# A graph network kernel: background list work moved from the ends of layers and the first attention batches into the steady stretches of layers 1 and 2

## The chip, the cores and the metric

The kernel runs on one core of a Trainium2 chip. The metric is device microseconds of one execution, lower is better. The inputs and the result lie in HBM. The engines are TensorE (PE; its weight loads are shown as PEld), VectorE (DVE), ScalarE (ACT), GpSimd (POOL) and SyncE (SP). Each engine works through its own queue of instructions in order. Plain DMAs are issued from the queues of SyncE and ScalarE; gathers and scatters by an index (indirect DMAs) are issued from GpSimd, one instruction for each 128 rows.

## The reference

A graph of 50000 nodes with 64 features and 25000 edges, sorted by target, goes through four layers. Each layer is `x = x + layer(relu(layernorm(x)))`.

```python
h = relu(layernorm(x)); m = relu(concat(h[src], h[dst]) @ W_msg + b_msg)        # layer 0
x = x + relu(concat(h, segment_mean(m, dst)) @ W_upd + b_upd)
h = relu(layernorm(x)); m = h[src] * (deg**-.5)[src] * (deg**-.5)[dst]          # layer 1
x = x + (segment_sum(m, dst) + h) @ W.T + b
h = relu(layernorm(x)); q, k, v = h @ Wq + bq, h @ Wk + bk, h @ Wv + bv         # layer 2, 4 heads
logits = sum(q[dst] * (k[src] + ek[type])) * scale + es[type] + clip(log(eg[type]))
agg = segment_sum((v[src] + ev[type]) * segment_softmax(logits, dst), dst) @ Wo + bo
y = layernorm(h + film(agg)); x = x + layernorm(y + gelu(y @ W1 + b1) @ W2 + b2)
h = relu(layernorm(x)); x = x + expm_multiply(h, src, dst, edge_weight, t)      # layer 3
```

Layer 3 applies a matrix exponential of the sparse edge matrix: 4 substeps of a Taylor series of 20 terms each.

## The kernel before, in words

**Tiling.** Nodes are cut into 49 batches of 1024 (`NQ`); the edges of a batch are put in 640 slots, five tiles of 128. Within a layer every batch goes through a list of stages (small Python functions), and the batches are staggered: in each round every batch that is under way runs its next stage, and then a new batch begins. Class `Steps` (from line 82) does a round, `pipeline` (line 110) repeats rounds until all 49 batches are through.

- Layer 0 (line 2229): `fetch, hots, message, sums, update, project`. `fetch` issues five gathers on GpSimd (`ga`), `project` ends with `g` (line 2222), which goes to the table `g1tab` in HBM.
- Layer 1 (line 2282): `fetch, scaled, sums, turn, product`. `fetch` issues five gathers `gt` from `g1tab`, into four buffers; `sums` adds the result to `x` (`x2`, line 2255); `product` writes the keys and values to `kvtab`.
- Layer 2 (lines 2499 to 2510): a pipeline `up` (`fetch, hots, logits`; five gathers `kvg` from `kvtab`) and a pipeline `down` of twelve stages, beginning with `fetch2, message, sums` and ending with `close`, which writes `h3tab`. The 49 batches form four groups (13, 12, 12, 12). First `up` runs alone over group 0, then a softmax over the group; after that `up` of the next group and `down` of the groups before it alternate. When all four softmaxes are done, `down` alone runs to its end.
- Layer 3 (from line 2631): a first power of the edge matrix, a second one, and then the powers 3 to 8 on short lists of edges, added to the output by GpSimd.

All of `g1tab`, `kvtab` and `h3tab` must be written before the next layer's first gather, since a batch may need any node.

**The list work.** The powers of layer 3 need, for each power k from 2 to 8, a list of those edges that continue a path. `build_lists` (from line 1920) is a Python generator that emits the instructions for these lists in small steps (`yield`). List 2 consists of 49 steps of five one-hot comparisons each (`lhot`, line 1791, VectorE, with nine small matmuls into a PSUM tile `lp`, line 1795), seven copies out of PSUM, 24 steps that mark nodes (line 1724), and 98 look-ups (`lgot`, one indirect DMA on GpSimd each). VectorE reads the look-ups in `llv` (lines 1733 and 1734). List 3 consists of 98 steps of one one-hot each (line 1878), eleven groups of key comparisons (`link`, line 1597), a marking (`map_three`) and 42 look-ups. Lists 4 to 8 are shorter, and each is a chain of scatter, reading back, comparing, scatter, look-up. `lhot` and `lp` have one buffer each. The whole is some 605 steps.

**How list work is let go.** An object `Pace` (line 121) hands it out. After every stage of a batch, the pipeline calls its hook; a call adds `rate` to a credit, and for each whole credit one step of the list work is emitted. Where a step yields "wait" (a DMA must land before the next), the credit is set to `-gap * rate`. `pipeline` can be given an `edge`: with `first=False`, the hook is used as long as batches are still begun, and once all 49 are begun each stage lets go `edge.edge` steps instead.

```python
        if edge:
            full = s.begun < len(items) and (not first or len(s.at) >= len(stages) - 1)
            s.hook = hook if full else lambda: edge(edge.edge)
```

In layer 0 the hook is another `Pace` called `work` (rate 0.1): weights of later layers, and `load_slots`, which loads the columns from which the lists start. It has 21 steps, which the first 210 of the 294 stages use up.

**Order of instructions.** The code gives an order, and the framework decides at build time the order in each engine's queue: an instruction whose inputs are ready can be put ahead of earlier code where its engine is planned to be idle. The queues on the chip are in order. So the position of a step in the code sets its rank, and not strictly its place.

Of the kernel before, what the change touches and what calls it, by code (L numbers as in the profile page):

```python
# [52 lines left out]
BK, NQ, RG = 392, 49, 98  # L53
# [56 lines left out]
def pipeline(items, stages, hook=None, edge=None, first=True):  # L110

    items = list(items)
    s = Steps(items, {q: State() for q in items}, stages, hook)
    while s.done < len(items):
# [3 lines that stand above are left out]
        s.step()  # L118
# [855 lines left out]
def fast(ctx: ExitStack, tc: tile.TileContext, a: dict, out: bass.AP, flag: bass.AP):  # L974
# [946 lines left out]
    def build_lists():  # L1921

        yield from list_two(cols)
        yield from list_three(lists[2])
        for k in range(4, KD + 1):
            q = lists[k - 1]
            yield from compact(k, q.live[:, :q.n], q.n, (q.src, q.dst, q.w.bitcast(I32), q.nextptr))

    lists_pace = Pace(build_lists())
# [77 lines left out]
    def halves(w, a0, a1, pool, name):  # L2007

        out = []
        for h in range(2):  # L2010
            t = pool.tile([P, D], F32, name=f"{name}{h}")
            nc.scalar.dma_start(t[0:D, :], (a0, a1)[h])
            nc.scalar.dma_start(t[D:P, :], (a1, a0)[h])
            out.append(t)
        return out
# [145 lines left out]
    with tc.tile_pool(name="l0c", bufs=1) as cp, tc.tile_pool(name="l0", bufs=2) as pool, \  # L2161
            tc.tile_pool(name="pl0", bufs=1, space=PSUM) as ps:
        wupd = halves(None, a["L0_gnn_W_upd"][D:2 * D, :], a["L0_gnn_W_upd"][0:D, :], cp, "wupd")
        bupd = bias_rows(cp, row_bcast("L0_gnn_b_upd", pool=cp), "bupd")
        w1t = cp.tile([P, P], F32, name="w1t")
        nc.vector.memset(w1t, 0.0)
        for h in range(2):
            nc.scalar.dma_start(w1t[h * D:(h + 1) * D, h * D:(h + 1) * D], a["L1_gnn_WT"])

        def fetch(q, s):  # L2170
            s.ga = pool.tile([P, 5, D], F32, name="ga", bufs=4)
            for i in range(5):
                gather(s.ga[:, i, :], atab, nrs[:, q, i:i + 1])
            s.bt = pool.tile([P, 8, BW], BF16, name="bt", bufs=4)
            nc.sync.dma_start(s.bt, nodes(btab, q))
            s.cat = pool.tile([P, 2, 512], F32, name="cat", bufs=5)
            load_turned(s.cat, h0t, q)
            s.xt = pool.tile([P, 8, D], F32, name="xt", bufs=6)
            load_x(s.xt, q)
            load_keys(pool, q, s)  # L2180

        def hots(q, s):
            node_hot(pool, s)
            s.soh = slot_hot(pool, key, q)

        def message(q, s):
            pe = ps.tile([P, 5, D], F32, name="pe", bufs=2)
            to_slots(pe, s, s.bt)
            z = pool.tile([P, 5, D], F32, name="z")
            nc.vector.tensor_add(z, s.ga, pe)  # L2190
            m3 = pool.tile([P, 5, 3, D], F32, name="m3")
            for i in range(5):
                nc.scalar.activation(m3[:, i, 0, :], z[:, i, :], AF.Relu, scale=cinv[:, q, i:i + 1])
            s.parts = split(m3)

        def sums(q, s):
            pa = ps.tile([P, 512], F32, name="pa")
            to_sums(pa, s.soh, s.parts)
            for h in range(2):
                r = slice(h * D, h * D + D)  # L2200
                nc.scalar.activation(s.cat[r, h, :], pa[r, :], AF.Copy)

        def update(q, s):
            po = ps.tile([P, 8, D], F32, name="po")
            bias_in(po.rearrange("p b d -> p (b d)"), bupd)
            for j in range(8):
                nc.tensor.matmul(po[:, j, :], s.cat[:, j // 4, j % 4 * P:j % 4 * P + P], wupd[j // 4],
                                 start=False, stop=(j == 7))
            s.x1 = pool.tile([P, 8, D], F32, name="x1", bufs=3)
            nc.vector.scalar_tensor_tensor(s.x1, po, 0.0, s.xt, op0=OP.max, op1=OP.add)  # L2210
            s.h = pool.tile([P, 8, D], F32, name="h")
            norm_relu(pool, s.h, s.x1)

        def project(q, s):
            tr = turned(pool, ps, s.h, "pt")
            pw = ps.tile([P, 8, D], F32, name="pw", bufs=2)
            for i in range(4):
                nc.tensor.matmul(pw[:, 2 * i:2 * i + 2, :].rearrange("p a d -> p (a d)"), tr[:, i, :], w1t,
                                 start=True, stop=True)
            g = pool.tile([P, 8, D], F32, name="g")  # L2220
            nc.vector.tensor_add(s.x1, s.x1, pw)
            nc.vector.tensor_mul(g, pw, over(disn[:, 8 * q:8 * q + 8], 8))
            nc.scalar.dma_start(nodes(x1tab, q), s.x1)
            nc.sync.dma_start(nodes(g1tab, q), g)

        work = Pace(itertools.chain(weights(), load_slots()), 0.1)
        next(work.work)
        lists_pace.edge = 5.0
        pipeline(range(NQ), (fetch, hots, message, sums, update, project), work, lists_pace, False)

# [1 line left out]
    with tc.tile_pool(name="l1", bufs=2) as pool, \  # L2234
            tc.tile_pool(name="pl1", bufs=1, space=PSUM) as ps:
        def fetch(q, s):
            s.gt = pool.tile([P, 5, D], F32, name="gt", bufs=4)
            for i in range(5):
                gather(s.gt[:, i, :], g1tab, nrs[:, q, i:i + 1])
            s.x1 = pool.tile([P, 8, D], F32, name="x1", bufs=4)  # L2240
            nc.sync.dma_start(s.x1, nodes(x1tab, q))

        def scaled(q, s):
            s.soh = slot_hot(pool, key, q)
            g3 = pool.tile([P, 5, 3, D], F32, name="g3")
            for i in range(5):
                nc.scalar.activation(g3[:, i, 0, :], s.gt[:, i, :], AF.Copy, scale=dise[:, q, i:i + 1])
            s.parts = split(g3)

        def sums(q, s):  # L2250
            po = ps.tile([P, 8, D], F32, name="po")
            bias_in(po.rearrange("p b d -> p (b d)"), b1l)
            to_nodes(po, s.soh, s.parts, started=True)
            x2 = pool.tile([P, 8, D], F32, name="x2")
            nc.vector.tensor_add(x2, s.x1, po)
            nc.scalar.dma_start(nodes(x2tab, q), x2)
            s.h2 = pool.tile([P, 8, D], F32, name="h2")
            norm_relu(pool, s.h2, x2)

        def turn(q, s):  # L2260
            s.tr = turned(pool, ps, s.h2, "pt")

        def product(q, s):
            kv = pool.tile([P, 8, 3 * D], F32, name="kv")
            q3 = pool.tile([P, 8, 3, D], F32, name="q3")
            for k in range(2):
                for h in range(2):
                    r = slice(h * D, h * D + D)
                    b = slice(4 * k + h, 4 * k + 4, 2)
                    pp = ps.tile([P, 2, 4 * D], F32, name="pp", bufs=4)  # L2270
                    for i in range(2):
                        nc.tensor.matmul(pp[:, i, :], s.tr[r, 2 * k + i, :], wkv[r, :], start=True, stop=True)  # L2272
                    nc.scalar.activation(kv[:, b, :], pp[:, :, :3 * D], AF.Copy)
                    nc.scalar.activation(q3[:, b, 0, :], pp[:, :, 3 * D:], AF.Copy)
            qt = pool.tile([P, 8, 3, D], BF16, name="qt")
            pack(q3, qt)
            nc.sync.dma_start(nodes(kvtab, q), kv[:, :, :2 * D])
            nc.sync.dma_start(nodes(h2tab, q), kv[:, :, 2 * D:])
            nc.scalar.dma_start(nodes(qtab, q), qt.rearrange("p b k d -> p b (k d)"))

        lists_pace.rate = 0.4
        pipeline(range(NQ), (fetch, scaled, sums, turn, product), lists_pace, lists_pace, False)


    with tc.tile_pool(name="l2", bufs=2) as pool, \
# [209 lines left out]
            nc.vector.scalar_tensor_tensor(h, s.xc, 0.0, over(invert(s, "r3"), 8), op0=OP.max, op1=OP.mult)  # L2495
            nc.scalar.dma_start(nodes(h3tab, q), h)

        lists_pace.rate, lists_pace.gap = 0.7, 5
        up = Steps(range(NQ), S, (fetch, hots, logits), lists_pace)
        down = Steps(range(NQ), S, (fetch2, message, sums, attend, spread1, turn, hidden, product, spread2, finish, spread3,  # L2500
                                      close), lists_pace)
        for k, (q0, n) in enumerate(batches):
            while up.done < q0 + n:
                up.step()
                if k:
                    down.step(q0)
            softmax(k)
        lists_pace.rate = 1.5
        while down.done < NQ:
            down.step(NQ)  # L2510
# [163 lines left out]
    sums = {}  # L2674
# [112 lines left out]
```

## Time and profile before

| what | value |
|---|---|
| runs | 3559.2, 3567.95 and 3574.22 us, median 3567.95 us |
| profiled execution, its own time | 3569.77 us |
| its span, first to last instruction | 3568.0 us |
| VectorE busy | 2620.7 us (73%), 8434 instructions |
| TensorE busy | 2492.4 us (70%) |
| GpSimd busy | 2070.2 us (58%), 1955 instructions |
| ScalarE busy | 1328.5 us (37%) |
| mean granted TensorE clock | 0.693 |
| layer 0's gathers `ga` | 656.9 to 1074.1 us |
| layer 1's gathers `gt` | 1185.6 to 1685.7 us |
| layer 2's gathers `kvg` | 1740.4 to 2471.0 us |
| layer 3's first gathers | from 2767.5 us |

The span is cut by these gathers into layers. A layer's length is the time from its first gather to the next layer's first gather. Busy shares are means over stretches with different limits, so the stretches are read one by one.

### The profile page before, as it was taken

The numbers are of one execution on the slowest core, as the hardware profiler recorded it, in microseconds if no ns is written. First come the engines' busy times: TensorE is split into PE (matmuls) and PEld (weight loads), VectorE is DVE, ScalarE is ACT, GpSimd is POOL, SyncE is SP. The second block draws the span as 40 slices with busy tenths as digits, with TensorE's granted clock in tenths as the row PEclk, the third lists the DMA queues.
The fourth block names the chain that finished last, engine by engine and source line by source line (L and its number), as shares of the span: only waits on it lengthen the run. The fifth ranks groups of instructions, "written<-read, shape, count | busy, mean of one in ns | idle before, by whom it ended". The sixth has DMA issues, their size and how long they took to land. (4 is left out here: it accounts for less than half of the span.)

```text
span 3568.0 us, 62333 instructions
## 1 busy us (share of the span) xinstructions
PE 2492.4 (70%) x21184; PEld 1729.4 (48%) x21184; DVE 2620.7 (73%) x8434; ACT 1328.5 (37%) x2962; POOL 2070.2 (58%) x1955
## 2 busy tenths in 40 slices
PE   7898675399987673477669779889888554356620
PEld 3324565266665452355446445555554443356520
DVE  9999998699998882488677877777878576456410
ACT  0002553144442262377204326646667333333000
POOL 0377777655550477665374127665430787775786
PEclk9755555699996575688657667777779775567555
DMA  1003783487771362478654234343233646377221
GB/s 54 6 4 90 205 234 123 110 224 212 211 200 44 90 197 75 130 234 243 188 145 124 62 90 132 111 122 110 80 94 101 211 139 193 96 216 213 45 26 12
DMA packets 530638, 463.35 MB, mean 130 GB/s; under 512 B 281171, under 2 KB 387954, under 8 KB 530180
## 3 DMA queue, kind: packets, MB, share of 16 engines
q1 hardware_dynamic: 365012, 269.33, 26.5%
q10 hardware_dynamic: 93408, 139.47, 11.3%
q0 software_dynamic: 71888, 50.46, 7.6%
q8 instruction: 169, 2.77, 0.3%
q14 instruction: 161, 1.32, 0.1%
HBM read 226.23 MB, written 233.89 MB: 129 GB/s over the span
## 5 line engine op out<-in xcount | busy, mean ns | idle before, releaser
L1013 POOL DMA_INDIRECT kvg<-kvtab,nrs x245 | 260.6, 1064 | 307.6 <-DVE es L2329 184.0
L1013 POOL DMA_INDIRECT gt<-g1tab,nrs x245 | 243.6, 994 | 238.6 <-DVE lhot L1791 110.6
L1013 POOL DMA_INDIRECT y<-h3tab,sptr x245 | 276.8, 1130 | 138.9 <-issue 68.0
L1013 POOL DMA_INDIRECT ga<-atab,nrs x245 | 250.3, 1022 | 170.4 <-DVE z L2190 60.5
L1991 PEld LDWEIGHTS <-soh 128*128 128x128 bf16 x4410 | 221.7, 117 | 237.0 <-issue 221.8
L1013 POOL DMA_INDIRECT raw<-otab,nrd x196 | 193.4, 987 | 191.9 <-DVE bad L1159 132.5
L1981 PE MATMUL pa<-soh,m 128*64 128x256 bf16 (+3 forms) x1764 | 238.9, 348 | 25.2 <-DVE m L1093 11.6
L1018 POOL DMA_INDIRECT stab<-raw,pf x196 | 207.3, 1058 | 59.8 <-issue 59.8
L1013 POOL DMA_INDIRECT lgot<-nmap,ldst x183 | 190.1, 1039 | 75.3 <-issue 52.8
L1991 PE MATMUL po<-g,soh 128*128 128x64 bf16 x2205 | 123.3, 215 | 145.5 <-DVE g L1093 143.0
L1950 DVE TENSOR_SCALAR soh<-it,key 128x512 bf16<-128x512 f16 (+2 forms) x735 | 210.7, 332 | 1.8 <-PE pa L1981 1.6
L1991 PE MATMUL po<-y,soh 128*128 128x64 bf16 x2205 | 122.3, 228 | 125.9 <-DVE y L1093 65.4
L2272 PE MATMUL pp<-wkv,tr 64*128 64x256 f32 x784 | 151.2, 496 | 52.4 <-ACT tr L2001 52.1
L1013 POOL DMA_INDIRECT y<-ftab,ldst x140 | 138.9, 992 | 75.0 <-issue 45.7
L1093 DVE TENSOR_TENSOR y<-y 128x320 f32<-128x320 f32 (+1 forms) x196 | 75.6, 389 | 140.6 <-ACT y L2617 116.3
L1942 DVE TENSOR_SCALAR noh<-keys,pblk 128x256 bf16<-128x256 f16 (+1 forms) x784 | 176.0, 286 | 2.8 <-DMA keys<-ktab 2.7
L1196 PE MATMUL pab<-wab,tr 64*128 64x128 f32 x784 | 150.3, 437 | 32.5 <-ACT tr L1183 32.5
L1981 PEld LDWEIGHTS <-m 128*64 128x64 bf16 x1764 | 118.0, 119 | 97.9 <-issue 32.5
L1196 PEld LDWEIGHTS pab<-wab,tr 64*128 64x128 f32 x784 | 136.3, 324 | 51.5 <-ACT tr L1183 51.5
L2338 PE MATMUL pe<-qt,noh 128*128 128x64 bf16 x2205 | 157.7, 231 | 0.3 <-DVE noh L1942 0.2
L2720 POOL DMA_INDIRECT out<-y,lnode x85 | 132.4, 1558 | 38.3 <-issue 24.4
L2617 ACT ACTIVATE y<-y,swgt 128x64 f32<-128x64 f32 x245 | 82.2, 345 | 176.6 <-DMA y<-h3tab,sptr 161.1
(607 smaller groups left out, 7496.8 us busy)
## 6 DMA issues: line engine op xcount, KB each, us to landing
kvtab<-kv SPq DMA_DIRECT2D x49, 512.0 KB
ftab<-f ACTq DMA_DIRECT2D x98, 256.0 KB
xt<-in_x SPq DMA_DIRECT2D x96, 256.0 KB
btab<-bt ACTq DMA_DIRECT2D x49, 384.0 KB
bt<-btab SPq DMA_DIRECT2D x49, 384.0 KB
qtab<-qt ACTq DMA_DIRECT2D x49, 384.0 KB
qt<-qtab SPq DMA_DIRECT2D x49, 384.0 KB
xs<-xstab SPq DMA_DIRECT2D x70, 256.0 KB
```

What stands on the lines that cost most here:

```text
L1013: return nc.gpsimd.indirect_dma_start(out=dst, out_offset=None, in_=tab[:, :], in_offset=IndirectOffsetOnAxis(ap=idx, axis=0))
L1018: return nc.gpsimd.indirect_dma_start(out=tab[:, :], out_offset=IndirectOffsetOnAxis(ap=idx, axis=0), in_=src, in_offset=None, bounds_chec ...
L1093: nc.vector.tensor_sub(x3[:, :, k, :], x3[:, :, k - 1, :], h[:, :, k - 1, :])
L1196: nc.tensor.matmul(pab[:, i, :], s.tr[r, i, :], wab[r, :], start=True, stop=True)
L1942: nc.vector.tensor_scalar(s.noh[:, j, :n * P], s.keys[:, t0 * P:(t0 + n) * P], pblk[:, j:j + 1], None, op0=OP.is_equal)
L1950: nc.vector.tensor_scalar(oh[:, OHW[i]:OHW[i + 1]], it16[:, b0 * P:(b0 + n) * P], keys[:, q, i:i + 1], None, op0=OP.is_equal)
L1981: nc.tensor.matmul(o, l, r, start=(k == 0), stop=(k == len(t) - 1))
L1991: nc.tensor.matmul(po[:, j, :], oh[:, c:c + P], msg[:, i, k, :], start=(not started and i == t0 and k == 0), stop=(end and (not started or ...
L2272: nc.tensor.matmul(pp[:, i, :], s.tr[r, 2 * k + i, :], wkv[r, :], start=True, stop=True)
L2338: nc.tensor.matmul(pe[:, i, :], s.noh[:, j, c:c + P], s.qt[:, j, k, :], start=False, stop=(j == b0 + nb - 1 and k == 2))
L2617: nc.scalar.activation(y3[:, i, 0, :], s.y[:, i, :], AF.Copy, scale=swgt[:, 5 * q + i:5 * q + i + 1])
L2720: st = nc.gpsimd.indirect_dma_start(out=out[:, :], out_offset=IndirectOffsetOnAxis(ap=s.node[:, t:t + 1], axis=0), in_=sums[k][:, t, :], i ...
```

## The change

Three rules for the list work are altered; no instruction is added or removed.

- At the end of layer 0 nothing of it is let go any more: `pipeline` gets no `edge`, and its hook is `work` to the end.
- In layer 1 the rate is 0.6 for each stage instead of 0.4, from the first to the last stage, and the last stages no longer let go five steps each.
- In layer 2 the rate is 0 during the first group and 0.75 afterwards, instead of 0.7 throughout. The rate of 1.5 once the four softmaxes are done stays.

```diff
         work = Pace(itertools.chain(weights(), load_slots()), 0.1)
         next(work.work)
-        lists_pace.edge = 5.0
-        pipeline(range(NQ), (fetch, hots, message, sums, update, project), work, lists_pace, False)
+        pipeline(range(NQ), (fetch, hots, message, sums, update, project), work)
...
-        lists_pace.rate = 0.4
-        pipeline(range(NQ), (fetch, scaled, sums, turn, product), lists_pace, lists_pace, False)
+        lists_pace.rate = 0.6
+        pipeline(range(NQ), (fetch, scaled, sums, turn, product), lists_pace)
...
-        lists_pace.rate, lists_pace.gap = 0.7, 5
+        lists_pace.rate, lists_pace.gap = 0.0, 5
         up = Steps(range(NQ), S, (fetch, hots, logits), lists_pace)
...
             softmax(k)
+            lists_pace.rate = 0.75
         lists_pace.rate = 1.5
```

## The prediction

> **What bounds the kernel now.** I read the strip of 40 slices first. It shows that no engine holds the whole span.
>
> ```profile
> DVE  9999998699998882488677877777878576456410
> POOL 0377777655550477665374127665430787775786
> ```
>
> VectorE (DVE) is at 8 or 9 in layer 0, but falls to 2 and 4 in slices 15 and 16 (1338 to 1516 us), where GpSimd (POOL) reads 6 and 7. Then I asked for the busy time by stretch, cut at the layers' ends. Columns: stretch, length, then busy us and instructions of PE, PEld, DVE, ACT, POOL; clock, DMA.
>
> ```profile
> 1094.00:1186.00 92.00, 68.10 (x547) 47.67 (x542) 74.30 (x318) 11.96 (x28) 0.38 (x1) 0.55 0.09 32
> 1186.00:1237.00 51.00, 32.32 (x326) 22.73 (x326) 41.48 (x183) 13.14 (x36) 38.67 (x40) 0.51 0.30 85
> 1237.00:1313.00 76.00, 64.69 (x636) 47.36 (x637) 67.97 (x198) 53.65 (x159) 48.66 (x43) 0.75 0.71 210
> 1313.00:1473.00 160.00, 43.83 (x404) 34.49 (x402) 41.88 (x103) 36.18 (x108) 119.84 (x126) 0.57 0.27 76
> 1473.00:1716.00 243.00, 176.48 (x2044) 141.39 (x2043) 208.79 (x499) 180.71 (x557) 134.21 (x135) 0.86 0.78 233
> ...
> 1740.00:1836.00 96.00, 65.37 (x792) 49.84 (x792) 62.62 (x286) 1.51 (x4) 74.21 (x71) 0.50 0.66 190
> ...
> 2545.00:2717.00 172.00, 154.24 (x806) 92.97 (x806) 140.20 (x475) 119.35 (x190) 48.03 (x45) 0.84 0.31 92
> ```
>
> Row 5 is layer 1 undisturbed: VectorE 86% busy, 31.8 batches in 243 us, so 7.64 us a batch with 1.1 us of VectorE idle. Row 1 is layer 0's end, row 2 layer 1's start, row 4 something that is not VectorE at all. The tile views say what. First the one-hots of list 2, then the look-ups `lgot`, and below them the gathers `gt`, in the stretches 1237 to 1313, 1313 to 1473 and 1473 to 1690.
>
> ```profile
> L1791 DVE TENSOR_SCALAR lhot<-it,lpos x245: 234/282/475, 1104.9 to 1204.9; 128x256 bf16<-128x256 f16 x123
> ...
> POOL gt L1013: 110.6, 1
> ```
>
> ```profile
> 1237.00:1313.00 76.00, 0.00 (x0) 21.38 (x18) 0.75 0.71 210
> 1313.00:1473.00 160.00, 0.21 (x1) 76.81 (x81) 0.57 0.27 76
> ```
>
> ```profile
> 1313.00:1473.00 160.00, 10.27 (x30) 43.03 (x45) 0.57 0.27 76
> 1473.00:1690.00 217.00, 47.11 (x139) 134.21 (x135) 0.87 0.80 238
> ```
>
> ```profile
> DVE llv L1733 <- DMA lgot<-nmap,ldst: 71.8, 1, 71.8
> ```
>
> The 245 one-hots lie across the change from layer 0 to layer 1. The look-ups stand between gathers, 81 to 45 in row 4's stretch: 126 indirect DMAs at 1.25 us each (0.95 busy, 0.30 to the next, by the timeline) make 158 of the 160 us. GpSimd is the bound there, and VectorE sits 71.8 us before `llv`, the last line, quoted from the waits of that stretch.
>
> **How many steps move.** Counting the code's credits through both versions gives, for layer 0's end, layer 1, layer 2's first group, the other groups, the end of `down`, layer 3: before 75, 132, 29, 282, 88, 0; after 0, 145, 0, 320, 140, 0. List 8 is done at the very end of layer 2 instead of 57 stages before that. Dense work of layer 3 begins at the same batch.
>
> **Part 1, layer 0's end.** `g` (line 2222) comes every 8.7 us up to 1096.5 us, and the last four at 1129.4, 1153.5, 1170.9 and 1181.7. In these 92 us the list's VectorE instructions, each counted to the start of the next, make 48.2 us, the rest 26.2, idle 17.6. Without the list, four more at 8.7 end at 1131: 50 us gained. Bounds: 60 if the end is limited by the 26 us left, 35 if the build fills the idle stretches with list work whose waits for `lp` stay. I take 48.
>
> **Part 2, list 2's VectorE work in layer 1.** It is 48.2 at layer 0's end, 26.8 in row 2 and 7.7 in row 3: 83 us. Some 18 us still find idle time (17.6 at layer 0's end, 9 at layer 1's start, less the waits). The other 65 go beside full batches. Row 3 prices that: nine batches in 75.6 us, 6.8 over nine times 7.64, for 7.7 us of list work, 0.9 for 1. So 58 us, of which today's layer 1 pays 23 (row 2: `x2` of batch 2 is 50 us after the first gather, where 13 to the first and 7.64 twice make 28) and 7. Loss: 28 us. Bounds by far rows: at 0.5, a loss of 2; at 1.5, the price of `link` and `map_three` (1991 to 2128 us: 137 us for four batches that take 17 each elsewhere, so 69 for 46.7 us of list work), a loss of 68.
>
> A rule speaks against this part. The Trainium skill, SBUF — State Buffer, section "Who interferes with whom", says that a `tensor_scalar` can run in a mode that takes a port pair which GpSimd needs to write its descriptors, and the later one blocks. The trace: beside 54 one-hots a gather took 0.967 us (row 2, 38.67 for 40), 0.956 in row 4 with VectorE mostly idle (43.03 for 45), 0.994 in row 5's. If each of the 245 blocked GpSimd for its whole 0.28 us, an estimate by the rule would be 69 us of GpSimd time; by these rows it is nothing that counts.
>
> **Part 3, the 98 look-ups.** The code before spreads them at two a batch from batch 7 to the end of layer 1. The trace has them at ten a batch, in 1278 to 1464 us: the build pulled them forward into GpSimd's idle places. The batches 13 to 17 took 153 us instead of 38: 115 us lost, about 98 times 1.25 less GpSimd's slack. After, the code has 57 of them from batch 28 of layer 1 on, three a batch, and 41 in layer 2. I expect them to be pulled forward again, as soon as list 2 is marked, ten a batch, with the same loss. Value 0; bounds: a gain of 68 (rival 1), a loss of 10.
>
> **Part 4, layer 1's end and the first group.** The 16 one-hots of list 3 leave the end of layer 1, where the last `qt` is 12 us behind the one before it instead of 7.6: 5 us gained (0 to 11). In the first group GpSimd's five gathers, 6.7 us a batch, end last (74.21 of 96 us busy, 0.30 between two), and VectorE has a third idle (row 6). So the 29 steps there cost nothing now, and 46 steps of list 3 (23 one-hots in the trace's first group, 7.5 us, 19 in the end of layer 1, 5.8 us, and their copies, some 4) go beside VectorE work of 17 us a batch: 15 us lost (0 to 25).
>
> **Part 5, `down`'s end.** 25 waits of lists fall there instead of 20. Today's thirteen batches take 13.2 us each, where those without list work lie 10.5 apart: 35 us, 1.75 a wait, 9 us for five. As many leave the groups before (12 to 8 waits): 7 back. Loss 2. Nothing hides the last steps, as `h3tab` must be complete for layer 3. Behind VectorE's reading of a look-up stand `finish` and `close` of the last batches; bounds 5 gained, 25 lost.
>
> **The sum.** −48 +28 +0 −5 +15 +2 = −8, so 3561 us from the profiled execution's own 3569.8 (its span and 1.8 around it, and 1.8 above the median of the runs). A measurement of this kernel can tell about 0.5% from no change, 18 us; this forecast lies within.
>
> **Rival 1, faster: the look-ups spread as the code has them.** If list 2's marking is late, its look-ups meet the end of layer 1 and the 53 us between the last `gt` and the first `kvg`, in which GpSimd is empty. Then 57 cost 71 us less 28 of slack, and 41 cost nothing: 43 instead of 111, and 3493 us. For it: three a batch is slow. Against: before, the look-ups ran at five times the rate of the code.
>
> **Rival 2, slower: list work in layer 1 at the price of `link`.** `lhot` and `lp` have one buffer, so each step goes from VectorE to TensorE and back, through two queues full of layer 1's work; whoever stands behind the waiting one-hot on VectorE (`ln_s`, `ln_xc`, `h`, and so `tr`, `pp`) waits with it. At 1.5 per us the 65 us cost 98, and the time is 3601. It decides from 1.2 on. For it: 1991 to 2128 us. Against: row 3, where marking by the same buffers cost 0.9.
>
> **Rival 3: it hardly does what it says.** The build pulls list 2 into the same idle places at layer 0's end, and all else with it: 3568.
>
> **How the numbers follow.** The forecast's case has 0.50, with 3535 to 3590 as its own range: 0.12 faster than 3550, 0.33 within, 0.05 slower than 3586. Rival 1 has 0.18, all faster; rival 2 0.25, all slower; rival 3 0.07, 0.06 of it within. Together 0.30, 0.39 and 0.31. The range reaches to both rivals with the outer part of each left out, and takes in the bounds of parts 3 and 5: 3505 to 3612.
>
> **What would show it.** Right: the first `gt` near 1138 us instead of 1185.6; batches of layer 1 10 us apart while list 2's one-hots run; 98 `lgot` in a block of some 150 us late in layer 1, ended by one long wait of `llv`; first group unchanged at 6.7 us a batch. Wrong: one-hots still ahead of the first `gt`; `lgot` in layer 2; batches over 12 us apart beside the one-hots; a first layer 3 gather that waits for a list.

## The result, and the profile after

| | before | changed |
|---|---|---|
| runs (median) | 3568.71 us | 3612.39 us |
| profiled execution, its own time | 3569.77 us | 3620.12 us |
| its span | 3568.0 us | 3618.2 us |
| mean granted TensorE clock | 0.693 | 0.688 |

The ratio is 1.012, with an interval of 1.0099 to 1.0141: 44 us slower, where 3561 had been forecast, and 0.4 us above 3612, the top of the range. Some of the experiments ran on chips where the kernel before itself takes 4674 to 4755 us and undisturbed batches of layer 1 lie 11.3 to 11.5 us apart; their numbers are marked "slower chips" below, and stand only against the kernel before beside them.

The layers, cut at the first gathers as before:

| us | before | changed | undone part 1 (`l0_back`, below) |
|---|---|---|---|
| up to the first `gt` | 1185.6 | 1132.6 | 1187.5 |
| layer 1, to the first `kvg` | 554.8 | 628.7 | 552.7 |
| layer 2, to the first `y` | 1027.1 | 1061.3 | 1010.2 |
| the rest | 800.5 | 795.7 | 794.7 |

Layer 0's end gave 53 us, layer 1 took 74 and layer 2 took 34. The strip of the changed kernel's page, the same two lines as before:

```profile
DVE  9999998699998777824677768787777576556310
POOL 0377777655553534676474211675352687765786
```

VectorE reads 7 in the slices 13 to 15 (1176 to 1447 us), where before had 8, 8 and 2. The hole of 2 and 4 is two slices later, and GpSimd's 7 and 6 with it. The stretches, columns as before (length, busy us and instructions of PE, PEld, DVE, ACT, POOL; clock, DMA share, GB/s):

```profile
1095.00:1133.00 38.00, 27.16 (x216) 19.52 (x215) 35.07 (x104) 10.98 (x27) 0.43 (x1) 0.80 0.22 76
1133.00:1198.00 65.00, 44.53 (x500) 33.56 (x500) 49.40 (x150) 35.74 (x106) 49.76 (x51) 0.67 0.59 170
1198.00:1442.00 244.00, 212.55 (x1643) 139.22 (x1642) 177.50 (x597) 117.82 (x347) 104.41 (x102) 0.56 0.52 149
1536.00:1677.00 141.00, 29.44 (x245) 22.30 (x246) 28.22 (x71) 25.30 (x74) 107.17 (x112) 0.57 0.22 57
```

Row 1 is layer 0's end: 38 us instead of 92. Row 4 is the look-ups' stall, with GpSimd as the bound: 141 us for four batches, 110 more than four times 7.64, where before lost 115. Row 3 is new. It is the stretch beside list 2's steps, as long as row 5 of before (243 us), but with 19 batches in place of 31.8: 12.8 us a batch, and 13.2 while the one-hots themselves run (14 batches in 1199 to 1384 us). VectorE is no longer full there (73%, against 86%). TensorE is busy for 87%, with a clock of 0.56 against 0.86. The tile views of list 2's one-hots and look-ups, and the wait that ends the look-ups:

```profile
L1791 DVE TENSOR_SCALAR lhot<-it,lpos x245: 230/281/434, 1125.9 to 1383.3; 128x256 bf16<-128x256 f16 x123
```

```profile
L1013 POOL DMA_INDIRECT lgot<-nmap,ldst x98: 940/944/1436, 1487.4 to 1669.8; - x98
```

```profile
DVE llv L1733 <- DMA lgot<-nmap,ldst: 81.6, 1, 81.6
```

The one-hots start where layer 0 ends and run for 257 us instead of 100. The look-ups still stand in a block, and VectorE still waits for its end. What VectorE waits for in 1199 to 1384 us (sum, times, longest):

```profile
DVE lhot L1791 <- PE lp L1795: 27.3, 20, 2.5
DVE ln_v L1138 <- ACT ln_sq L1151: 21.1, 13, 2.4
DVE lkey L1799 <- PE lp L1795: 3.7, 3, 2.5
```

For 31 us the next one-hot, or the copy behind a group, waits for TensorE's list matmuls into `lp`. Before has no such wait in its undisturbed stretch, which holds next to no list work.

The waits of the other engines in row 3 lead to TensorE too:

```profile
POOL gt L1013 <- ACT g L2246: 104.6, 17, 12.1
ACT kv L2272 <- PE pp L2271: 80.5, 56, 2.7
```

ScalarE's copies `kv` wait 80.5 us for TensorE's product `pp`. The gathers wait 104.6 us until ScalarE's `g` has freed their buffer, 5.5 us a batch. In the undisturbed stretch of before they wait 1.2 a batch for it (39.6 us), and no copy waits for `pp`. So the batches of row 3 wait for TensorE at two places, VectorE for `lp` and ScalarE for `pp`.

### The profile page after: what moved, and what is told of

The parts are those of the page before. It is cut to its first block, busy times and chain, and to the rows that moved or that the text cites. A ratio compares the mean times of both kernels' runs of the same rounds, so it can differ in the third digit from the quotient of the medians.

```text
span 3618.2 us, 62349 instructions
## 1 busy us (share of the span) xinstructions
PE 2534.7 (70%) x21184; PEld 1745.6 (48%) x21184; DVE 2618.7 (72%) x8434; ACT 1325.6 (37%) x2955; POOL 2061.2 (57%) x1955
## 5 line engine op out<-in xcount | busy, mean ns | idle before, releaser
L1013 POOL DMA_INDIRECT y<-h3tab,sptr x245 | 267.9, 1093 | 92.8 <-issue 70.4
L1981 PE MATMUL pa<-soh,m 128*64 128x512 bf16 (+3 forms) x1764 | 230.6, 344 | 29.9 <-DVE m L1093 13.0
L2271 PE MATMUL pp<-wkv,tr 64*128 64x256 f32 x784 | 218.8, 559 | 29.5 <-ACT tr L2001 29.4
L2271 PEld LDWEIGHTS pp<-wkv,tr 64*128 64x128 f32 x784 | 127.7, 265 | 60.2 <-ACT tr L2001 44.5
L2337 PE MATMUL pe<-qt,noh 128*128 128x64 bf16 x2205 | 150.0, 227 | 0.3
```

Of the source, the lines that this page charges most:

```text
L1013: return nc.gpsimd.indirect_dma_start(out=dst, out_offset=None, in_=tab[:, :], in_offset=IndirectOffsetOnAxis(ap=idx, axis=0))
L1981: nc.tensor.matmul(o, l, r, start=(k == 0), stop=(k == len(t) - 1))
L2337: nc.tensor.matmul(pe[:, i, :], s.noh[:, j, c:c + P], s.qt[:, j, k, :], start=False, stop=(j == b0 + nb - 1 and k == 2))
```

## The experiments

Three explanations of the 13 us a batch are set against each other. Hand-off: VectorE's one-hots and TensorE's list matmuls wait for each other through the one buffer between them. Clock: the list's small matmuls lower TensorE's granted clock, and TensorE then bounds the batches, with or without a hand-off. Plain load: VectorE only has more to do.

**The changed kernel again, and part 1 undone.** Two kernels on one chip. The first is the changed kernel as it is:

> The changed kernel as it is, beside the kernel before on one more chip: where the kernel before takes about 3569 us, 1.010 to 1.014 as first measured. The runs so far had 4736 us for the kernel before, with TensorE's results reaching VectorE and ScalarE later than the trace of before has them. On such a chip the clock theory (layer 1 lost its time since TensorE fell to half clock beside list 2's steps) expects less than +20 us, since layer 1's undisturbed batches take 11.3 us there anyway and TensorE has nothing to lose; the price of the hand-off or of plain VectorE load expects the +44 us or more to stay.

It ran where the kernel before takes 3573 us: 3611.22 us, ratio 1.0109 (1.0092 to 1.0126). Its profile repeats the first one (layer 1 627.9 us, layer 2 1058.6); what the change does on a slower chip, it could not show. The second has layer 0's end as before and all else as changed:

```diff
-        pipeline(range(NQ), (fetch, hots, message, sums, update, project), work)
+        lists_pace.edge = 5.0
+        pipeline(range(NQ), (fetch, hots, message, sums, update, project), work, lists_pace, False)
```

> The changed kernel with part 1 undone: five steps a stage beside layer 0's end again, so that list 2's one-hots and most flags are done before layer 1. Layer 1 (three steps a batch, none at its end) and layer 2 (none in the first batch, then 0.75) stay as changed. Layer 0's end then costs its 50 us again, and layer 1's 18 batches at 13 us are gone. Clock or hand-off theory, on a chip like that of the first traces: layer 1 gets shorter by 65 to 90 us, the kernel by 15 to 40 against the changed one, so 3575 to 3600. By the prediction's own terms (layer 0's end -48, VectorE work +28): slower than the changed kernel by about 20 us.

Measured: 3546.92 us, 0.9929 of before (0.9912 to 0.9945), and 64 us below the changed kernel. This is more than any theory had, and the sign of my own terms was wrong. The table above has its layers. Against the second profile of the changed kernel, on the same chip, it has 57 us more up to the first `gt`, 75 less in layer 1 and 48 less in layer 2. So part 1 costs twice: in layer 1, and again in layer 2. The same kernel beats both: what is left of the change (no list work in layer 2's first group, 0.6 in layer 1 to its last stage, 0.75 later) gains 26 us.

**Real steps, no steps and dummies in one layer.** The changed kernel, in which layer 1 has 35 dummy steps behind list 2's one-hots, after six batches without. A dummy step has the same instructions, but its comparisons go into a tile that nobody reads, and its matmuls take a constant. Both are held to a place, behind the last `x2` and the last bias matmul.

```diff
+        yield from itertools.chain(itertools.repeat(None, 18), load(True, True))
         has = lw.tile([P, CAP[2]], F32, name="lhas")
...
+                with tc.issue_after(latest["vector"].ins):
+                    for i in range(5):
+                        hot = lc.tile([P, 2 * P], BF16, name="dhot")
+                        nc.vector.tensor_scalar(hot, it16[:, :2 * P], pidx, None, op0=OP.is_equal)
...
+                            nc.tensor.matmul(po[:, 2 * (q % PG) + o, :], hotc[:, o * P:(o + 1) * P], hotc[:, :NF],
+                                             start=(i == o), stop=(i == 4))
```

> The changed kernel, and in the same layer 1 behind list 2's one-hots, after six batches without list steps, 35 dummy steps at the same three a batch: five comparisons on VectorE and nine narrow matmuls on TensorE each, nothing passing between them, before the flags and look-ups go on. It adds some 12 batches of load, and all later list steps come later; to be read are three stretches of the same layer, not the total: batches beside real steps, batches without, batches beside dummies. Hand-off theory: the dummies' batches are shorter than the real steps' by 2 us or more. Clock theory, or plain load: both the same within 0.7 us; then the clock theory has TensorE over 85% busy in both and its granted clock under 0.65 where undisturbed batches had 0.86, plain load has VectorE over 85% busy and the clock kept.

It took 3659.21 us, beside 3567.93 for before. The three stretches of its layer 1, in the order real steps, none, dummies:

```profile
1199.00:1386.00 187.00, 161.40 (x1339) 107.66 (x1340) 141.77 (x476) 93.48 (x276) 86.38 (x84) 0.61 0.54 156
1386.00:1440.00 54.00, 41.38 (x521) 32.48 (x519) 53.09 (x152) 41.42 (x124) 33.20 (x32) 0.77 0.82 234
1440.00:1573.00 133.00, 101.43 (x1139) 79.19 (x1137) 119.64 (x391) 77.83 (x234) 70.63 (x70) 0.73 0.65 187
```

They hold 15, 7 and 13 batches by the `x2` additions: 12.5, 7.7 and 10.2 us a batch (the first 22 dummy comparisons already run at the end of the second stretch). VectorE's load of list work per batch is the same. The real stretch has 40.5 us of list work on VectorE (2.7 a batch), the other 36.2 (31.5 of 153 dummies and 4.7 of the list's own, 2.8 a batch). Over batches of 7.64 us that makes 72.4 us for 40.5, or 1.8 per us, with the hand-off, and 33.7 for 36.2, or 0.93 per us, without it. VectorE's waits in the first and the third stretch:

```profile
DVE lhot L1791 <- PE lp L1795: 23.5, 20, 2.7
DVE ln_v L1138 <- ACT ln_sq L1151: 15.5, 11, 2.3
DVE lkey L1799 <- PE lp L1795: 3.6, 3, 2.5
...
DVE x L2283 <- PE po L2020: 9.2, 10, 1.4
DVE ln_v L1138 <- ACT ln_sq L1151: 2.5, 6, 1.3
```

Its waits for the list's own matmuls are 27.1 us in 15 batches, 1.8 a batch. Beside the dummies 1.4 us of such waits are left in all, for the few marking steps of the list itself. The batches differ by 2.2 us. This is the hand-off theory's forecast (2 us or more), and my clock theory, by which the load alone lowers the clock, falls for this chip: the same load without the hand-off leaves the clock at 0.73, near the 0.77 without list work, and VectorE is 90% busy. The clock of 0.61 goes along with the hand-off. How much of the 2.2 us the low clock adds, by letting TensorE's matmuls end later, is not separated here: the waits of ScalarE's `kv` for `pp` fall as well, from 57.7 us in 15 batches to 30.0 in 13. The dummies are also held to their place, which the real steps are not, and what that does by itself was not tried. All three stretches are from one execution.

**The two loads one by one (slower chips).** On the changed kernel list 2's steps were finished beside layer 0 (six a stage), and 49 dummy steps took their place in layer 1. First both loads, then the comparisons alone, then the matmuls alone:

```diff
+        lists_pace.work = itertools.chain(itertools.repeat(None, 15), load(True, True), lists_pace.work)
         lists_pace.rate = 0.6
```

> This kernel takes list 2's one-hots and flags out of layer 1: they are finished at the end of layer 0, six steps to a stage. In their place layer 1 runs 49 dummy steps, three a batch as in the changed kernel, each with five 128x256 comparisons on VectorE into a tile that nobody reads, and nine 128x128x7 matmuls on TensorE with a constant one-hot. So both engines have the load of list 2's steps, and nothing passes from one to the other. Three theories on why layer 1's batches went from 7.64 to 13.4 us apart beside list 2's steps, at a granted clock of 0.56 in place of 0.86. Clock: the steps' narrow matmuls slow the stream until the granted clock falls, and TensorE at half clock becomes the bound; it needs no hand-off, so here the batches lie over 12 us apart with the clock under 0.65. Hand-off: the comparisons and matmuls wait for each other through the one buffer between them, which is gone here, so the batches lie at 9.5 to 10.5 us, the clock at 0.75 or more. Plain VectorE load (2.6 us a batch): 10.2 us or so as well, VectorE above 85% busy.

> As the kernel with both dummy loads, but only the five 128x256 comparisons a step stay, three steps a batch; the dummy matmuls are left out. Clock theory: without the extra matmuls the stretch stays near the undisturbed one, 8 to 10.5 us a batch, the clock above 0.7; if the gaps that VectorE's load leaves on TensorE are enough to drop the clock, 12 us or more. Hand-off: 9.5 to 10.5 us. Plain VectorE load: 7.64 + 2.6 = 10.2 us, the same as with both dummies.

> As the kernel with both dummy loads, but only the nine narrow matmuls a step stay (27 a batch, and one 14-column copy to seven steps); the dummy comparisons are left out. Clock theory: the granted clock falls below 0.65 and the batches lie over 10 us apart though VectorE has hardly any added work. Hand-off and plain VectorE load: 7.6 to 8.2 us a batch, clock about 0.85, since 27 matmuls of some 60 ns are 1.6 us on an engine that is 5.55 us busy in 7.64.

Totals 4742.69, 4766.1 and 4735.86 us, beside 4674.26 for before. The batches of a stretch beside the dummies lie 13.5 us apart with both loads (10 batches, 2091 to 2226 us), 13.7 with the comparisons (12 in 164 us), 11.5 with the matmuls (12 in 138 us), and 11.3 with none (15 in 170 us). The stretches with the comparisons alone, and of the third kernel with the matmuls and with neither:

```profile
2099.00:2263.00 164.00, 76.63 (x793) 62.18 (x792) 113.59 (x375) 72.85 (x217) 59.78 (x60) 0.75 0.47 138
```

```profile
2070.00:2208.00 138.00, 88.73 (x1121) 74.22 (x1121) 83.15 (x211) 71.52 (x217) 59.79 (x60) 0.73 0.56 164
2264.00:2434.00 170.00, 98.40 (x990) 81.11 (x990) 101.11 (x241) 89.19 (x270) 74.63 (x75) 0.74 0.57 166
```

So the narrow matmuls cost almost nothing and keep the clock (0.73 against 0.74), and the comparisons cost 2.3 us a batch, though VectorE is only 69% busy with them. With both loads the clock reads 0.63 in its stretch, and the batches are still no longer than with the comparisons alone. Since the undisturbed batches are longer there, this does not settle the question for the first chips. Three more runs of the kernel with both loads, on other slower chips:

> The same kernel as d_free (dummy comparisons and dummy narrow matmuls, nothing passing between them, in the place of list 2's one-hots in layer 1), to be read against the profiles of before and after: batches of 7.64 us at clock 0.86 without list work, 13.4 us at 0.56 with list 2's steps. Clock theory: over 12 us a batch, clock under 0.65, TensorE over 85% busy. Hand-off: 9.5 to 10.5 us, clock 0.75 or more, since there is none here. Plain VectorE load: about 10.2 us, VectorE over 85% busy.

> The dummy loads (five comparisons a step on VectorE, nine narrow matmuls a step on TensorE, three steps a batch, nothing passing between them; list 2's own steps are done beside layer 0's end) once more, where the kernel before takes about 3570 us. Undone part 1 gave 0.993 of before, 65 us off the changed kernel: the time is lost beside list 2's steps in layer 1. Clock theory: the dummies do the same, batches over 12 us apart, clock under 0.65, TensorE over 85% busy. Hand-off theory: 9.5 to 10.5 us and clock 0.75 or more, since here nothing is handed over. Plain VectorE load: about 10.2 us, VectorE over 85% busy.

> The dummy loads of list 2's steps with nothing handed over (five comparisons on VectorE and nine narrow matmuls on TensorE a step, three steps a batch, list 2's own steps done beside layer 0's end), to be read where the kernel before takes about 3570 us and undisturbed batches of layer 1 take 7.64 us at clock 0.86; there list 2's real steps made them 13.4 us at 0.56. Clock theory: over 12 us a batch, clock under 0.65, TensorE over 85% busy. Hand-off theory: 9.5 to 10.5 us and clock 0.75 or more. Plain VectorE load: about 10.2 us, VectorE over 85% busy.

Totals 4771.83, 4741.07 and 4745.72 us, beside 4735.92, 4737.03 and 4687.39 for before, and 13.8, 13.6 and 13.4 us a batch over twelve batches, where the first has 13.6 by the same count and undisturbed batches 11.4 to 11.5. They confirm the first, and like it they do not speak for the first chips.

**More columns for TensorE (slower chips).** The changed kernel with a filler behind each matmul of the product:

```diff
                         nc.tensor.matmul(pp[:, i, :], s.tr[r, 2 * k + i, :], wkv[r, :], start=True, stop=True)
+                        nc.tensor.matmul(fill, ident16, it16[:, :512], start=True, stop=True)
```

> The changed kernel with eight filler matmuls a batch in layer 1 (128x128 by 512 columns, bf16, into a PSUM bank of their own that nobody reads), one behind each matmul of the product. It only adds work to TensorE. Clock theory: the filler's columns open the gate, the granted clock in the stretch of list 2's one-hots rises to 0.8 or more, the batches come down from 13.4 to 11 us or less, and layer 1 gets shorter by 20 us or more. Hand-off theory or plain load: no gain, 13 us a batch or more, and layer 1 the same or longer by the added 1.7 to 3.4 us a batch.

> The changed kernel with eight filler matmuls of 512 columns a batch in layer 1, once more, where the kernel before takes about 3570 us. Clock theory, if a denser stream can open the clock: the granted clock in the stretch of list 2's one-hots rises from 0.56 to 0.8 or more, batches of 11 us or less in place of 13.4, the kernel shorter than the changed one by 20 us or more. Clock theory, if it can't, and hand-off theory: the filler (1.7 us a batch at full clock, 3.4 at half) is added, 15 to 17 us a batch at the low clock or 13 to 15, and the kernel is longer by 40 us or more.

> The changed kernel with eight filler matmuls of 512 columns a batch in layer 1, to be read where the kernel before takes about 3570 us. Clock theory, if a denser stream can open the clock: granted clock from 0.56 to 0.8 or more in the stretch of list 2's one-hots, batches of 11 us or less in place of 13.4, the kernel shorter than the changed one (3611) by 20 us or more. Clock theory, if it can't, and hand-off theory: the filler (1.7 us a batch at full clock, 3.4 at half) is added, 15 to 17 us a batch at the low clock or 13 to 15 at a high one, and the kernel is longer by 20 us or more.

4746.73, 4802.91 and 4813.59 us, against 4674, 4737 and 4740 for before: longer each time. The question was what the clock alone is worth at 13 us a batch. The changed kernel without the filler was not run on these chips, so there is nothing to set these times against, and the question stays open.

**One part alone (slower chips).** Part 1 alone, on the kernel before:

> The kernel before with part 1 of the change alone: nothing let go beside layer 0. Layer 1 keeps two steps a batch (rate 0.4) and its end, layer 2 its rates. List 2's one-hots so lie beside some 25 full batches of layer 1, at two thirds of the changed kernel's density. By the prediction's terms: 48 us gained at layer 0's end, VectorE load of 65 us at 0.9 back, less the 30 us paid today, list 3 later by some 40 steps: -20 to +15 us. By the price of the hand-off (1.5 us per us): +20. By the clock: if two steps a batch are enough to drop the granted clock to 0.56, batches of 11 to 12 us with TensorE over 85% busy and +30 to +50; if the clock holds at 0.8 or more, batches of 9 to 10 us and no loss.

4703.76 us, 0.9922 (0.9899 to 0.9946): faster. Against the next kernel, whose layers 0 and 1 are those of before, the first `gt` is at 1719.1 us instead of 1768.5, the 49 us of part 1; layer 1 has 709.8 us instead of 737.4, and layer 2 1318 instead of 1279. So there the later lists cost layer 2 some 39 us too (the next kernel's other rates in layer 2 did not change its total beyond its interval), but layer 1 does not pay. This does not carry over to chips with 7.64 us a batch, where it was not run. Layer 2's rates alone:

> The kernel before with the change's rates in layer 2 alone: no step in the first batch of layer 2, then 0.75 a stage in place of 0.7. Layers 0 and 1 are as before. The prediction priced this at -5 to +25, taking +2: the five waits of the last lists that lie in the last stages and the steps that move there. The profile of the changed kernel has 41 us more between the last softmax and the first gather of layer 3, and 32 us more from the first gather of layer 2 on. If the later lists do that, +20 to +40 here. If it came from layer 1's later lists or its clock, within 10 us of before.

4737.59 us, 1.0 (0.998 to 1.002). So the rates by themselves do not make the kernel longer there; on the first chips the kernel with part 1 undone says the same, since it has these rates and a layer 2 of 1010 us.

**The look-ups held to their place (slower chips, no gain).** The kernel before with each look-up of list 2 behind the gathers of its batch, at a rate of 0.2; then the same on the kernel with part 1 undone:

```diff
+                with tc.issue_after(latest["gather"].ins):
+                    gather(got[:, t:t + 1], nmap, s.dst[:, t:t + 1])
```

> The kernel before, its rates and its work beside layer 0's end kept, with one thing changed: each of list 2's 98 look-ups is held behind the five gathers of the layer-1 batch beside which the code has it, one look-up a batch (40 of them), and the other 58 come after layer 1's last gather. In the trace of before these look-ups were pulled forward, ten to a batch, and the stretch from 1353 to 1473 us lost about 111 us to them. If that loss is the price of the crowd in GpSimd's queue (prediction, part 3), one look-up fits into the 1.4 us that GpSimd has free in a batch of 7.64 us, layer 1's end of about 50 us hides most of the other 58, and the kernel gets 65 to 95 us shorter. If the look-ups themselves are what costs (1.1 us each wherever they stand, on a queue that bounds the layer), it stays within 20 us of before.

> The kernel before with list 2's look-ups held to their place in the code, one a batch, the other 58 behind layer 1's last gather. Where the kernel before takes 4736 us this gave 1.0009: the batches, 11.3 us apart without look-ups, went to 12.9 with one. Where it takes about 3570 us: if one look-up fits into the 1.4 us that GpSimd has free in 7.64 us, layer 1 loses 111 us of stall, its end takes some 10 to 20 us more for the 58, and the kernel takes 3480 to 3510. If each look-up costs its 1.25 us of GpSimd's queue wherever it stands, 40 x 1.25 = 50 in the batches and the rest at the end: 3540 to 3575.

> Two things together on the changed kernel: part 1 undone (five steps a stage beside layer 0's end), and the look-ups of list 2 held to one a batch, 58 of them at layer 1's end; layer 2 as changed (none in its first batch, then 0.75). Part 1 undone took 3547 us. If the pinned look-ups hide, 65 to 90 us less: 3455 to 3485. If each costs its 1.25 us of GpSimd's queue, within 20 us of 3547.

> Part 1 undone and the look-ups of list 2 held to one a batch, 58 of them behind layer 1's last gather; layer 2 as changed. Where the kernel before takes 4737 us this gave 1.0024. Where it takes about 3570 us, part 1 undone alone gave 3547. If the pinned look-ups hide in the 1.4 us that GpSimd has free in a batch of 7.64 us and in layer 1's end, 65 to 90 us less: 3455 to 3485. If each costs its 1.25 us of GpSimd's queue, within 20 us of 3547.

The kernel before so altered had 1.0009 (0.9987 to 1.0031) and 0.9974 (0.9948 to 0.9999) of before; the other 1.0024 (0.9996 to 1.0052) and 0.9997 (0.9981 to 1.0013). Nothing is gained against before; part 1 undone without this was not run on these chips. One look-up a batch took the batches from 11.4 to 12.8 us, although GpSimd has some 5 us free in each; and beside the 58 at the end one batch comes 77 us after the one before it. VectorE's longest waits at the end of layer 1, from the first run of the kernel before so altered:

```profile
DVE x L2262 <- PE po L1998: 38.9, 2, 38.1
DVE q L1100 <- issue: 29.7, 1, 29.7
```

VectorE waits there with layer 1's last batches behind it. Whether spread look-ups would hide on the first chips is open.

## Why the prediction was wrong

**Part 1, right.** 48 us forecast, 53 found (55 in the second profile), within the bounds. The first `gt` was to come near 1138 us and came at 1132.6.

**Part 2, the step that failed.** The sum took 0.9 us per us of list work from row 3 of before. That agrees with the price of VectorE time without a hand-off (0.93 beside the dummies). Row 3 held only 7.7 us of list work in nine batches, so that a step could wait for `lp` without the next one being due (argued, not tried). At three steps a batch, 39.6 us of list work in 1199 to 1384 us made 185 us out of 14 times 7.64 = 107: 1.97 per us, and batches 13.2 us apart where 10 had been expected and over 12 had been named as a sign of being wrong. Layer 1 as a whole is 74 us longer, where parts 2 and 4 together had 23. Rival 2 named the hand-off, though not the clock, and its time, 3601, is nearest to the 3612 found; even its 1.5 per us was low. The profile of before had the warning in the stretch beside `link`, which I took for the far row. Rival 1 fell, since the look-ups came in a block again, and rival 3, since the first `gt` did move.

**No term for the clock.** The sum carried every engine's durations over from before. TensorE's matmuls `pp` had a median of 376 ns in the undisturbed stretch of before and have 631 ns in row 3 of after (in each line the shortest, the median and the longest in ns):

```profile
L2272 PE MATMUL pp<-wkv,tr x494: 376/376/793, 1472.7 to 1715.6; 64*128 64x256 f32 x165
```

```profile
L2271 PE MATMUL pp<-wkv,tr x304: 376/631/793, 1198.0 to 1435.9; 64*128 64x256 f32 x152
```

Beside the dummies the clock stayed at 0.73, where the real steps of the same execution had 0.61. So on that chip the load alone does not bring it down; the low clock came with the waiting. On a slower chip both dummy loads had 0.63 without a hand-off, so this does not hold for every chip. A sum with fixed durations holds neither the waits nor the clock.

**Part 3, right.** 98 look-ups in a block late in layer 1, ended by one long wait of `llv`, with 110 us lost instead of 115.

**Part 4, probably the wrong sign.** Moving list 3's steps out of the first group was priced at 15 us lost. The first three groups of layer 2 by stretch, columns as above, of before and then of the kernel with part 1 undone:

```profile
1740.00:1852.00 112.00, 67.61 (x807) 51.27 (x807) 77.98 (x320) 3.53 (x6) 86.86 (x82) 0.50 0.59 172
1852.00:2050.00 198.00, 164.84 (x1316) 105.96 (x1315) 153.30 (x636) 70.87 (x101) 70.00 (x64) 0.70 0.35 101
2050.00:2309.00 259.00, 222.12 (x1444) 134.07 (x1444) 203.09 (x700) 133.37 (x191) 150.47 (x144) 0.70 0.38 112
```

```profile
1740.00:1847.00 107.00, 64.14 (x749) 48.58 (x747) 74.41 (x291) 3.91 (x7) 81.96 (x82) 0.50 0.67 182
1847.00:2021.00 174.00, 151.08 (x1303) 96.25 (x1303) 137.61 (x536) 71.57 (x100) 65.99 (x63) 0.76 0.39 111
2021.00:2291.00 270.00, 225.18 (x1458) 138.11 (x1456) 217.48 (x795) 130.13 (x188) 146.50 (x135) 0.70 0.36 105
```

The first group gets 5 us shorter, the second 24 with 100 VectorE instructions fewer, and the third 11 longer. The first group was not free of cost after all, and the last two stretches of the layer change by −5 and +6: 17 us gained in all. That kernel also lets go 0.6 a stage in layer 1, so the 17 us are not shown to come from the empty first group alone; the rates of layer 2 alone were run on the slower chips only, and changed nothing.

**Part 5, mis-sized by a missing link.** `down`'s end was priced at +2 from the counts of waits. It became 262 us instead of 221. With the same rates but list 2 on time it is 227. The stretch from the last softmax to layer 3's first gather, of before, of the changed kernel, and with part 1 undone:

```profile
2546.00:2767.00 221.00, 186.90 (x949) 111.36 (x948) 177.88 (x551) 150.28 (x240) 48.03 (x45) 0.83 0.31 97
```

```profile
2560.00:2822.00 262.00, 200.75 (x964) 121.07 (x962) 188.82 (x638) 154.94 (x244) 90.50 (x87) 0.77 0.28 83
```

```profile
2523.00:2750.00 227.00, 196.08 (x949) 113.64 (x947) 179.39 (x555) 153.84 (x241) 47.54 (x45) 0.81 0.31 95
```

Twice as many GpSimd instructions fall into the changed kernel's stretch (87 against 45), and VectorE waits 36.8 us for the look-ups and scattered rows of the last lists there, against 10 before. From the changed kernel's waits in that stretch:

```profile
DVE lpi L1619 <- DMA lgot<-nmap,ldst: 25.6, 4, 8.5
...
DVE lsrc L1573 <- DMA lback<-lrow: 11.2, 3, 7.7
```

The lists are a chain: list 2's look-ups ended at 1671 us instead of 1464, and of these 207 us 101 arrive at the last look-up of all (2804 us instead of 2703), where nothing hides it. The counts gave the steps of each stretch, but not this.

Put together, the measured terms are −53 for layer 0's end, +74 for layer 1, +34 for layer 2 and −5 for the rest, 50 us between the two profiled spans.

## What to carry to other kernels

Price side work beside a full pipeline by what it hands over, not only by its busy time: a step that goes from one engine to another and back through one buffer cost 1.8 to 2.0 us per us of its work here, the lower clock beside it included, and the same load without the hand-off 0.93. Work that fills an idle end of a stage for 50 us can still be cheap, if it would cost 75 beside the next stage. And when a chain of dependent work starts late, look for its last link: the delay shows up where nothing is left to cover it.

## What the runs showed of the hardware

- TensorE was 87% busy over 244 us at a mean granted clock of 0.56, and 73% busy over 243 us at 0.86 in before. A high busy share did not bring a high clock. The Trainium skill, TensorE: Matmul & The Clock Gate, section "What's actually happening", says that the clock is set by how busy the array has been recently; the busy shares of the profile alone do not order the clocks of these stretches.
- Beside the one-hots a gather took 1.02 us (104.41 for 102 instructions), against 0.96 in the look-ups' stretch (107.17 for 112). That is at most some 7 us of GpSimd's time in a stretch where it is idle for 140, so the port rule that the prediction weighed did not decide here either.
- On the slower chips a look-up added to a batch cost 1.4 us, though GpSimd was idle for 5 of 11.4 us.
